# Output projection of a half chunk by seven block products, with shared row buffers and a new first chunk

## The chip, the cores and the metric

The kernel runs on one core of a Trainium2 chip, as one launch. The metric is device time in microseconds; three runs of the kernel before took 1395.66, 1396.66 and 1398.48 us, median 1396.66 us.

## The reference

The input x is 8 sequences of 1024 rows with 512 features, all float32. The reference does one attention sublayer and one feed-forward sublayer, each with a layer norm before and after and a residual:

```python
Q, K, V = heads(ln(x) @ Wq.T + bq), ...        # 16 heads of 32 columns
scores = Q @ K.T / sqrt(32) - (i - j)          # causal; the decay falls by 1 a row
out = softmax(scores) @ V @ Wo.T + bo          # <- the projection that is changed
x = x + ln(out)
xh = ln(x) @ H                                 # Hadamard, 512 x 512
xq = round(xh / s) * s                         # 4 bits, s from the row's maximum
x = x + ln(xq @ ternary(W).T)
```

The output projection is 8192 rows by 512 by 512, plain float32.

## The kernel before

Because the decay falls by 1 per row, only the own block of 128 keys and the block before it matter, and the fast path `band()` keeps only these (a general path stands behind a flag that the data decides). The work is cut into 16 chunks of 512 rows; a chunk has four tiles of 128 rows and two halves of 256 rows. Three kinds of work run side by side:

- **Attention units.** A chunk has eight, one per half and group of four heads. A unit is `scores` (TensorE into the four PSUM banks of `s`, L571, and four exponentials on ScalarE, L585), `mask` and `add_keys` (GpSimd, L596 and L610), `values` (TensorE into the single bank `av`, L626 and L637) and `divide` (VectorE, L655 to L660), which writes four heads of `oT`, the transposed attention output of the half.
- **Q, K and V of the next chunk.** Class `Projections`. Each of the three is already done as a two-by-two block product with seven instead of eight block multiplications (the Strassen-Winograd scheme): `Weight.combine` and `replace` make the weight combinations once, `Projections.combine` makes four combinations `T` of the input on GpSimd per chunk, `product` does one of the seven (L417, four matmuls of 128x256), `drain` adds it to what it belongs to (mostly VectorE, L447 to L470).
- **The rest of a tile.** Generator `rest`, 64 times: the output projection (`project`, L153, four matmuls of 128x512 into `o_ps`), the addition of the bias on VectorE (`y`, L187), its statistics, `x1` (L194), the Hadamard transform (`u` and `w` on VectorE, L198 to L203, four transposes `wT` on TensorE, L210, then `h_ps`, L218), the quantisation (`sc`, `isc`, `qf`, `qi`, L238 to L248), transposes `qiT` (L255), the ternary matmul `f_ps` (L153), statistics and the second residual on GpSimd (L285). `norm_in` is the same kind of generator for the first layer norm of chunks to come (`xc`, `xn`, `xnT`, L133 to L146).

The order is written out by hand. One turn of the loop over `u` handles two units, five or six of the 21 products, one tile's norm and the first and second part of one rest each (`rest_a`, `rest_b`). The engines take their instructions in this order. Three PSUM banks (`held`, `one`, `two`, chosen by `bank`) serve products, projections and transposes; the same bank is used again only after its content was read. A row buffer with `bufs=1` is likewise written only after its last reader.

A float32 matmul appears in the profile as two matmul records, called passes below. Before the loop, the first chunk's V, K and Q are computed by plain products of 128x512 (`project_v`, `project_qk`), while VectorE and GpSimd prepare the weights (`prepare`, `Weight.combine`).

Of the kernel before, what the change touches and what calls it, by code (L numbers as in the profile page):

```python
# [40 lines left out]
def sandwich_kernel(  # L41
# [88 lines left out]
    def norm_in(pools, row0, xnT, t, name):  # L130
# [6 lines left out]
        xn = pools.row.tile([P, D], F32, tag="xn", name=f"xn_{name}", bufs=1)  # L137
# [29 lines left out]
    def rest(pools, n, row0, oT, warm=(0, 0, 0), last=False):  # L167
# [13 lines left out]
        xr = row.tile([P, D], F32, tag="xr", name=f"xr_{n}", bufs=2)  # L181
        nc.sync.dma_start(xr, xf[row0, :])
        yield
        ps = project(pools, f"o_{n}", oT, lambda k: wo_sb[:, k, :])
        yield
        y = row.tile([P, D], F32, tag="y", name=f"y_{n}", bufs=1)
        nc.vector.tensor_tensor(y, ps, bo2, ALU.add)  # L187
# [9 lines left out]
        u = row.tile([P, D], F32, tag="u", name=f"u_{n}", bufs=1)  # L197
# [13 lines left out]
        wT = row.tile([P, KD, P], F32, tag="wT", name=f"wT_{n}", bufs=1)  # L211
# [33 lines left out]
        qf = row.tile([P, D], F32, tag="qf", name=f"qf_{n}", bufs=1)  # L245
        nc.scalar.activation(qf, xh, AF.Identity, bias=round_col, scale=isc)
        qi = row.tile([P, D], BF16, tag="qi", name=f"qi_{n}", bufs=1)
# [8 lines left out]
        qiT = row.tile([P, KD, P], BF16, tag="qiT", name=f"qiT_{n}", bufs=1)  # L256
# [47 lines left out]
    def band():  # L304
# [11 lines left out]
        class Chunk:  # L316
            def __init__(self, at):
                self.at = at
                self.b, self.c = divmod(at, NCHUNK)
                self.n = f"{self.b}_{self.c}"  # L320
                self.rests = []
# [54 lines left out]
        class Projections:  # L376


            ORDER = (1, 2, 6, 7, 5, 4, 3)

            def __init__(self, ch, before):
                self.ch, self.before, self.done, self.undrained = ch, before, 0, []
                ch.qT = big.tile([P, KD, CT], F32, tag="qT", name=f"qT_{ch.n}")
                ch.kT = big.tile([P, KD, CT], F32, tag="kT", name=f"kT_{ch.n}")
                ch.v = big.tile([P, TPC, D], F32, tag="v", name=f"v_{ch.n}")

            def combine(self, which, engine=nc.gpsimd):
# [4 lines left out]
                if which == 0:  # L392
# [4 lines left out]
                    self.parts = {1: b11, 2: b21, 3: b22, 5: t[:, 0], 6: t[:, 1]}  # L397
                elif which == 1:
                    nc.gpsimd.tensor_tensor(self.t[:, 2], b22, b12, ALU.subtract)
                    self.parts[7] = self.t[:, 2]  # L400
                else:
                    nc.gpsimd.tensor_tensor(self.t[:, 3], self.t[:, 1], b21, ALU.subtract)
                    self.parts[4] = self.t[:, 3]
# [18 lines left out]
            def drain(self):  # L422
# [11 lines left out]
                if which == 1:  # L434
                    self.u = row.tile([P, HB, HW], F32, tag="u2", name=f"u2_{name}", bufs=2)
# [69 lines left out]
            def shift(self):  # L505
# [5 lines left out]
                nc.gpsimd.tensor_scalar(shift, shift, -SLACK, -0.5, ALU.mult, ALU.add)  # L511
                nc.gpsimd.tensor_scalar(shift, shift, ROUND, None, ALU.add)
                nc.gpsimd.tensor_scalar(shift, shift, ROUND, None, ALU.subtract)
                ch.bias = small.tile([P, 2, 2], F32, tag="bias", name=f"bias_{ch.n}")
                nc.gpsimd.tensor_scalar(ch.bias, decay_cols, shift, None, ALU.add)
# [14 lines left out]
        class Unit:  # L530
# [118 lines left out]
            def divide(self):  # L649
# [8 lines left out]
                rn = row.tile([P, nblk, HD], F32, tag="rn", name=f"rn_{self.n}", bufs=1)  # L658
# [15 lines left out]

        def start_rest(ch, t):
# [10 lines left out]
                left == 1,  # L686
            )

# [8 lines left out]
        weights = [Weight(w, n) for w, n in ((wq_sb, "wq"), (wk_sb, "wk"), (wv_sb, "wv"))]  # L697

# [7 lines left out]
        ch.kT = big.tile([P, KD, CT], F32, tag="kT", name=f"kT_{ch.n}")  # L706
        ch.qT = big.tile([P, KD, CT], F32, tag="qT", name=f"qT_{ch.n}")
        ch.v = big.tile([P, TPC, D], F32, tag="v", name=f"v_{ch.n}")
# [19 lines left out]
        def squares_of_q(o0, o1):  # L728
            nc.scalar.activation(sqq[:, o0:o1, :], ch.qT[:, o0:o1, :], AF.Square)
# [9 lines left out]
        first = Projections(ch, None)  # L739
        prep = prepare(pools, wf_sb)  # L740
        ahead_steps = {0: "01", 1: "02", 2: "0", 3: "132", 4: "1", 5: "23", 6: "2", 7: "3", 8: "3"}
        for i in range(3 * KD):
            if i % 2 or not i:
                for t in ahead_steps.get(i, ""):
                    next(ahead_norms[int(t)])
            which, o = divmod(i, KD)
            if which == 0:
                project_v(pools, wv_sb, ch.v, ch.xnT, o, ch.n)
            elif which == 1:
                project_qk(pools, "k", wk_sb, bk_sb, ch.kT, ch.xnT, o, ch.n)  # L750
            else:
                project_qk(pools, "q", wq_sb, bq_sb, ch.qT, ch.xnT, o, ch.n)
            if i == 0:
# [3 lines left out]
            elif i == 1:  # L757
                transposed(3)
            elif i == KD - 1:
                prepare_q(wq_sb)  # L760
                nc.gpsimd.tensor_tensor(bqk_step[:, 0], bq_sb[:, HB:], bq_sb[:, :HB], ALU.subtract)
                nc.gpsimd.tensor_tensor(bqk_step[:, 1], bk_sb[:, HB:], bk_sb[:, :HB], ALU.subtract)
                weights[2].combine()
                weights[2].replace()
                weights[1].combine()
            elif i == 2 * KD - 1:
                weights[0].combine()
                weights[1].replace()
                sqk = squares(ch, "k", ch.kT)
                sqq = row.tile([P, KD, CT], BF16, tag="sq", name=f"sqq_{ch.n}", bufs=1)  # L770
            elif i == 2 * KD:
                ch.mk = largest_of(ch, "k", norms_of(ch, "k", sqk))
            elif i == 2 * KD + 2:
                squares_of_q(0, HB)
            if i and i % 2 == 0:
                for t in ahead_steps.get(i, ""):
                    next(ahead_norms[int(t)])
            if i in (KD, 6, 2 * KD):
                next(prep)
        squares_of_q(HB, KD)  # L780
        next(prep)
        next(prep)
        ch.mq = largest_of(ch, "q", norms_of(ch, "q", [sqq[:, o, :] for o in range(KD)]))
        first.multiply()
        next(prep)
        first.shift()
        next(prep)
        weights[0].replace(nc.vector)
# [22 lines left out]
        def bank(at):  # L811
            pools.ps_m.named = at

# [5 lines left out]
        for at, ch in enumerate(chunks[:-1]):  # L819
# [7 lines left out]
            for u in range(0, 2 * NG, 2):  # L827

                new = Unit(ch, before, u)
                new.scores()  # L830
                if u == 0:
                    proj.combine(0, nc.gpsimd if at else nc.vector)
                if unit:
                    unit.values()
                    unit.divide()
                unit = new
                steps(rest_a, 1)
                if u >= 4:
                    proj.square()
# [5 lines left out]
                norm = next(norms_due)  # L845
                steps(norm, 1)
# [7 lines left out]
                if u == 0:  # L854
                    proj.combine(1)
                rest_a = next(rests_due) if at or u >= 4 else None
                bank(one)
                steps(rest_a, 1)
                bank(two)
                steps(rest_b, 1)  # L860
                steps(rest_a, 1)
# [4 lines left out]
                new = Unit(ch, before, u + 1)  # L866
                new.scores()
                unit.values()
# [4 lines left out]
                steps(rest_b, 1)  # L873
# [3 lines left out]
                if u == 0:  # L877
                    proj.combine(2)
                steps(rest_a, 1)
                proj.drain()  # L880
                steps(rest_b, 1)
                new.add_keys()
                if u < 6:
                    unit.divide()
                bank(one)
                steps(norm, 1)
                bank(two)
                proj.product()
                proj.drain()
# [3 lines left out]
                if u == 6:  # L893
# [11 lines left out]
                    held, two = two, held  # L905
                else:
# [9 lines left out]
                steps(rest_a, 2)  # L916

# [252 lines left out]
    def prepare(pools, wf_sb):  # L1170
# [4 lines left out]
        nc.vector.tensor_reduce(ws, w, AX.X, ALU.add, apply_absolute_value=True)  # L1175
# [5 lines left out]
        diag = row.tile([P, KD, P], F32, tag="u", name="wdiag", bufs=1)  # L1181

        def ternary(k):
            below = row.tile([P, D], F32, tag="y", name=f"below_{k}", bufs=1)
            nc.vector.tensor_scalar(below, w[:, k, :], lo[:, k : k + 1], None, ALU.is_lt)
            tern = row.tile([P, D], BF16, tag=("qi", "qiT")[k % 2], name=f"tern_{k}", bufs=1)
            nc.vector.scalar_tensor_tensor(
                tern, w[:, k, :], hi[:, k : k + 1], below, ALU.is_gt, ALU.subtract
# [4 lines left out]
            return tern  # L1193

        def transposed(k, tern):
            pt = pools.ps_m.tile([P, KD, P], BF16, tag="pm", name=f"ternT_ps_{k}")
            for i in range(KD):
                nc.tensor.transpose(pt[:, i, :], tern[:, i * P : (i + 1) * P], ident_bf)
            nc.vector.tensor_copy(ternT[:, :, k * P : (k + 1) * P], pt)

        terns = [ternary(k) for k in range(2)]
        yield
        for k in range(2):
            transposed(k, terns[k])
        terns += [ternary(k) for k in range(2, KD)]
        yield
        nc.vector.tensor_copy(had0_sb, had_sb)
        nc.vector.memset(had0_sb[:, 0:1], 0.0)
        bvw = row.tile([P, KD, P], F32, tag="wT", name="bvw", bufs=1)
        nc.vector.tensor_copy(bvw, bvT_sb.unsqueeze(2).to_broadcast([P, KD, P]))  # L1210
# [4 lines left out]
        yield  # L1215
        for k in range(2, KD):
            transposed(k, terns[k])
        yield
        ps = pools.ps_m.tile([P, D], F32, tag="pm", name="bo2_ps")
# [59 lines left out]
```

## Time and profile before

| | us |
|---|---|
| median of three runs | 1396.66 |
| the profiled execution's own time | 1396.07 |
| its span, first to last instruction | 1394.3 |
| first `s` of the loop / last turn of the loop ends | 61.94 / about 1296 |

| engine | busy us | share |
|---|---|---|
| PE | 1363.4 | 98% |
| DVE | 1015.7 | 73% |
| POOL | 892.0 | 64% |
| ACT | 681.2 | 49% |

PE is TensorE, DVE is VectorE, ACT is ScalarE and POOL is GpSimd. Busy time of PE counts a matmul from its start to its modelled end, and consecutive matmuls overlap, so the distance from one start to the next tells more than the mean duration. The mean granted TensorE clock is 0.995.

### The profile page before, as it was taken

Reading aid. Unit: us, or ns where it says so; the run is one execution under the profiler, and the core shown is the slowest. Engines: PE = TensorE matmul, PEld = TensorE weight load, DVE = VectorE, ACT = ScalarE, POOL = GpSimd, SP = SyncE. Lnnn points to the kernel's source line nnn. Section 1 sums busy time; section 2 is a strip of 40 time slices with the busy share of each in tenths; the row PEclk is TensorE's granted clock in tenths of the full one; section 3 lists DMA queues with packets and bytes.
Section 4 is the critical chain, followed back from the end, with each engine's and each line's share of the span. In section 5 each row is a group of like instructions: output and inputs, shape, how many; then the busy total and the mean of one; then the engine's idle time right before and its main releaser. Section 6 shows DMA issues by size and latency. Waiting matters only on the chain.

```text
span 1394.3 us, 35003 instructions
## 1 busy us (share of the span) xinstructions
PE 1363.4 (98%) x14504; PEld 967.5 (69%) x14504; DVE 1015.7 (73%) x2167; ACT 681.2 (49%) x1176; POOL 892.0 (64%) x1280
## 2 busy tenths in 40 slices
PE   9999999999999999999999999999999999999895
PEld 5577777777767777767776777777776777766553
DVE  5467777777777776777777777877777777777675
ACT  3345454545445455554545545445544545535442
POOL 4565758576576767658676676757757666665434
PEclk9999999999999999999999999999999999999998
DMA  6010011011011011011011011011101101000010
GB/s 228 8 47 24 24 47 46 24 47 47 24 47 47 24 47 47 32 39 47 30 41 46 25 47 47 28 43 47 40 31 47 47 24 47 25 23 32 32 39 33
DMA packets 31750, 58.23 MB, mean 42 GB/s; under 512 B 4064, under 2 KB 4448, under 8 KB 31584
## 3 DMA queue, kind: packets, MB, share of 16 engines
q1 hardware_dynamic: 30720, 54.87, 11.4%
q8 instruction: 116, 1.90, 0.5%
q10 hardware_dynamic: 864, 1.05, 0.2%
q14 instruction: 50, 0.41, 0.1%
HBM read 39.13 MB, written 16.78 MB: 40 GB/s over the span
## 4 chain that ended last, share of the span: by engine, by line


## 5 line engine op out<-in xcount | busy, mean ns | idle before, releaser
L585 ACT ACTIVATE pr<-s,bias 128x512 f32<-128x512 f32 (+1 forms) x512 | 295.3, 660 | 138.5 <-PE s L571 138.5
L610 POOL TENSOR_TENSOR both<-pr 128x1024 f32<-128x1024 f32 (+1 forms) x120 | 250.5, 2088 | 5.2
L153 PE MATMUL o_ps<-wo_sb,oT 128*128 128x512 f32 x512 | 236.1, 604 | 0.6
L596 POOL TENSOR_SCALAR_AFFINE_SELECT pr<-pr 128x1024 f32<-128x1024 f32 x128 | 150.0, 1172 | 108.2 <-ACT pr L585 103.8
L153 PEld LDWEIGHTS o_ps<-wo_sb,oT 128*128 128x128 f32 x512 | 93.2, 192 | 95.2 <-issue 92.5
L187 DVE TENSOR_TENSOR y<-o_ps,bo 128x512 f32<-128x512 f32 x64 | 44.2, 691 | 150.5 <-PE o_ps L153 150.5
L626 PE MATMUL av<-pr,v 128*32 128x128 f32 (+1 forms) x2816 | 130.7, 316 | 1.8 <-DVE oT L660 1.8
L571 PE MATMUL s<-qT,kT 32*64 32x192 f32 (+2 forms) x5632 | 119.9, 285 | 1.5 <-ACT pr L585 1.5
L571 PEld LDWEIGHTS s<-qT,kT 32*64 32x64 f32 x5632 | 99.8, 131 | 31.0 <-issue 21.6
L141 ACT ACTIVATE xn<-xc,nmr,rstd_n 128x512 f32<-128x512 f32 x60 | 48.8, 814 | 140.0 <-POOL nmr L139 140.0
L119 POOL TENSOR_SCALAR rstd_a<-mv_a 128x1 f32<-128x1 f32 x64 | 13.9, 217 | 142.7 <-DVE mv_a L127 141.5
L226 ACT ACTIVATE wT<-h_ps 128x512 f32<-128x512 f32 x64 | 38.2, 597 | 133.8 <-PE h_ps L218 133.8
L626 PEld LDWEIGHTS av<-pr,v 128*32 128x32 f32 x2816 | 74.9, 110 | 35.4 <-issue 1.8
L212 ACT COPY wT<-wT_ps 128x512 f32<-128x512 f32 x64 | 37.5, 585 | 123.4 <-PE wT_ps L210 123.4
L238 DVE TENSOR_REDUCE sc<-h_ps 128x1 f32<-128x512 f32 x64 | 44.1, 689 | 63.8 <-ACT wT L226 63.8
L119 POOL TENSOR_SCALAR rstd_c<-mv_c 128x1 f32<-128x1 f32 x64 | 14.7, 229 | 116.1 <-DVE mv_c L127 116.0
L285 POOL TENSOR_TENSOR y<-y,x 128x512 f32<-128x512 f32 x63 | 80.6, 1279 | 1.3 <-ACT y L284 1.3
L637 PE MATMUL av<-both,ones 128*32 128x256 f32 x960 | 74.2, 381 | 0.5 <-POOL both L614 0.5
L218 PEld LDWEIGHTS h_ps<-had_sb,wT 128*128 128x128 f32 x512 | 66.8, 192 | 6.2 <-ACT wT L212 3.3
L218 PE MATMUL h_ps<-had_sb,wT 128*128 128x128 f32 x512 | 68.1, 276 | 2.1 <-ACT wT L212 2.1
L153 PE MATMUL f_ps<-ternT,qiT 128*128 128x512 bf16 x256 | 66.2, 382 | 2.4 <-ACT qiT L257 2.4
L146 ACT COPY xnT<-xnT_ps 128x512 f32<-128x512 f32 x60 | 35.2, 586 | 56.8 <-PE xnT_ps L145 56.8
(213 smaller groups left out, 3100.7 us busy)
## 6 DMA issues: line engine op xcount, KB each, us to landing
xr<-in_x SPq DMA_DIRECT2D x64, 256.0 KB, 2.9
out<-y SPq DMA_DIRECT2D x63, 256.0 KB, 2.0
xc<-in_x SPq DMA_DIRECT2D x60, 256.0 KB, 2.7
wv_sb<-in_wvT ACTq DMA_DIRECT2D x4, 256.0 KB, 5.1
x<-in_x SPq DMA_DIRECT2D x4, 256.0 KB, 4.9
wk_sb<-in_wkT SPq DMA_DIRECT2D x1, 1024.0 KB, 6.7
wq_sb<-in_wqT SPq DMA_DIRECT2D x1, 1024.0 KB, 9.0
wf_sb<-in_wf SPq DMA_DIRECT2D x1, 1024.0 KB, 10.7
```

The lines of the kernel that those rows point to most:

```text
L141: nc.scalar.activation(xn, xc, AF.Identity, bias=nmr, scale=r)
L153: nc.tensor.matmul(ps, lhs(k), rhs(k), start=(k == 0), stop=(k == KD - 1))
L187: nc.vector.tensor_tensor(y, ps, bo2, ALU.add)
L218: nc.tensor.matmul(xh[:, k * P : (k + 1) * P], wT[:, k, :], had_sb if k else had0_sb, start=True, stop=True,)
L238: nc.vector.tensor_reduce(sc, xh, AX.X, ALU.max, apply_absolute_value=True)
L285: nc.gpsimd.tensor_tensor(y2, y2, x1, ALU.add)
L571: nc.tensor.matmul(s[half * hp : (half + 1) * hp, hh, column[which] + c0 : column[which] + c1], kc.kT[hsl, g, k0 : k0 + hp], ch.qT[hsl, g, ...
L585: nc.scalar.activation(pr[:, :, r0:, own, cols], s5[:, :, r0:, own, cols], AF.Exp, bias=ch.bias[:, own, h : h + 1],)
L596: nc.gpsimd.affine_select(out=own, in_=own, compare_op=ALU.is_ge, fill=0.0, base=0, pattern=[[0, HPG], [0, 2], [1, P]], channel_multiplier=-1,
L610: engine.tensor_tensor(self.both[:, :, r0:], pr[:, :, r0:, 0, :], pr[:, :, r0:, 1, :], ALU.add)
L626: nc.tensor.matmul(av[hh * HD : (hh + 1) * HD, 0, qc : qc + w], kc.v[:, at, h * HD : (h + 1) * HD], pr[:, hh, sc : sc + w], start=(at_part ...
L637: nc.tensor.matmul(av[hh * HD : (hh + 1) * HD, 1, :], ones[:, :HD], self.both[:, hh].rearrange("p r c -> p (r c)") if own is None else sel ...
```

## The change

Both tiles of a half are now projected together. The half's `oT` is 512 by 256, so as blocks it is two by two (two halves of the features, two tiles), and `wo` is two by two as well. A class `Output` makes four combinations of `oT`: `t0`, `t1` and one in place of a block on GpSimd, one in place on VectorE. It does seven products of two matmuls of 128x256, and puts them in pairs into one PSUM bank: 1 and 2, 6 and 7, 4 and 5, then 3 alone. Nine additions of 128x256 on VectorE per half lay them into `y` of the two tiles. All seven products stand in the first half of every second turn (`pair`), where the old order had one tile's projection; one of the Q, K and V products goes from each `pair` turn to the turn after it. 29 of the 32 halves are done like this; the last six tiles keep the plain projection, for which `wo` is loaded a second time.

```diff
+            def combine(self, which):
+                if which == 0:
+                    self.t0 = row.tile([P, HB, P], F32, tag="t0", ...)
+                    nc.gpsimd.tensor_tensor(self.t0, self.b12, self.b11, ALU.subtract)
+                elif which == 1:
+                    self.t1 = row.tile([P, HB, P], F32, tag="t1", ...)
+                    nc.gpsimd.tensor_tensor(self.t1, self.b22, self.t0, ALU.subtract)
+                    nc.gpsimd.tensor_tensor(self.b12, self.b22, self.b12, ALU.subtract)
...
+                else:
+                    nc.vector.tensor_tensor(self.b21, self.t1, self.b21, ALU.subtract)
...
+            def drain(self, which):
...
+                if which == 1:
+                    add(self.u, ps, bo2[:, left], ALU.add)
+                elif which == 2:
+                    add(self.y[0][:, left], ps, self.u, ALU.add)
+                elif which == 6:
+                    add(self.u, ps, self.u, ALU.add)
+                    add(self.u3, self.u, bo2[:, right], ALU.add)
+                elif which == 7:
+                    add(self.u3, ps, self.u3, ALU.add)
+                elif which == 4:
+                    add(self.y[0][:, right], ps, self.u3, ALU.add)
+                elif which == 5:
+                    add(self.y[1][:, right], ps, self.u3, ALU.add)
+                    add(self.u, ps, self.u, ALU.add)
+                else:
+                    add(self.y[1][:, left], ps, self.u, ALU.add)
```

`rest` takes the finished `y` instead of projecting. Rows with a short life share buffers: `u`, `wT` and `qf` one, `qi` and `qiT` one, `xn` and `w` one, `sumT` and `rn` one; `xr`, `u2` have one buffer instead of two, and the load of `xr` is issued one step later.

```diff
-        xn = pools.row.tile([P, D], F32, tag="xn", name=f"xn_{name}", bufs=1)
+        xn = pools.row.tile([P, D], F32, tag="w", name=f"xn_{name}", bufs=1)
...
-        xr = row.tile([P, D], F32, tag="xr", name=f"xr_{n}", bufs=2)
+        yield
+        xr = row.tile([P, D], F32, tag="u3" if last else "xr", name=f"xr_{n}", bufs=1)
         nc.sync.dma_start(xr, xf[row0, :])
-        yield
-        ps = project(pools, f"o_{n}", oT, lambda k: wo_sb[:, k, :])
-        yield
-        y = row.tile([P, D], F32, tag="y", name=f"y_{n}", bufs=1)
-        nc.vector.tensor_tensor(y, ps, bo2, ALU.add)
+        if not made:
+            ps = project(pools, f"o_{n}", oT, lambda k: wo_sb[:, k, :])
+        yield
+        if made:
+            y = made()
+        else:
...
```

The loop over `u`, in its first half:

```diff
                 if unit:
                     unit.values()
                     unit.divide()
+                if out:
+                    out.combine(1)
...
                 bank(one)
-                steps(rest_a, 1)
-                bank(two)
-                steps(rest_b, 1)
-                steps(rest_a, 1)
+                if out:
+                    out.products(1, 2)
+                    steps(rest_a, 1)
+                    out.drain(1)
+                    out.drain(2)
+                    bank(held)
+                    steps(rest_b, 1)
+                    out.combine(2)
+                    steps(rest_b, 1)
+                    bank(two)
+                    out.products(6, 7)
+                    out.drain(6)
+                    out.drain(7)
+                    bank(one)
+                    out.products(4, 5)
+                    out.drain(4)
+                    steps(rest_a, 1)
+                    out.drain(5)
+                    bank(held)
+                    steps(norm, 1)
+                    bank(two)
+                    out.products(3)
+                    out.drain(3)
+                else:
+                    if not pair:
+                        proj.product()
+                        proj.drain()
...
```

In the second half of a turn `new.add_keys()` (GpSimd) goes ahead of a step of `rest_b`, and in a `pair` turn the transposes `xnT` are no longer there and one product is left out. The products of Q, K and V come in the order 1, 2, 6, 7, 5, 3, 4. `Projections.combine(0)` on GpSimd moves behind the first unit's `add_keys`. `wo.combine` and `wo.replace` (GpSimd) come in the first chunk, between turns.

Ahead of the loop, K and Q of the first chunk are done by seven products each, with the input combinations on VectorE; the absolute sums of the ternary weights go from one VectorE reduction to four ScalarE instructions; the bias row `bvw` is summed over the four blocks of features on GpSimd (seven instructions of 128x512), so that one matmul in place of four is left; and the ternary preparation is spread between the products, one or two VectorE instructions at a time:

```diff
+        for i in range(kinds):
+            first.product()
+            first.drain()
...
+            next(prep)
+        sqk = squares(ch, "k", ch.kT)
...
```

## The prediction

> **What bounds the kernel now.** I read first the page (busy times), then the groups of instructions with shapes kept apart, then who waited for whom on PE and DVE, and last the timeline of one turn in the steady part.
>
> ```profile
> PE 1363.4 (98%) x14504; PEld 967.5 (69%) x14504; DVE 1015.7 (73%) x2167; ACT 681.2 (49%) x1176; POOL 892.0 (64%) x1280
> ...
> L153 PE MATMUL o_ps<-wo_sb,oT 128*128 128x512 f32 x512 | 236.1, 604 | 0.6
> L417 PE MATMUL q_ps<-xnT,wq_s 128*128 128x256 f32 x120 | 28.4, 379 | 0.0
> ```
>
> TensorE is busy 98% of the span and the output projection is its largest group. So TensorE's work is the bound, if it really works in that time. The waits say that it does:
>
> ```profile
> PE qiT_ps L255 <- DVE qi L248: 4.4, 6, 1.1
> PE f_ps L153 <- ACT qiT L257: 2.4, 3, 1.0
> ...
> DVE y L187 <- PE o_ps L153: 150.5, 60, 5.7
> ```
>
> The longest entry of PE is 4.4 us in all, while VectorE waits 150.5 us for the output projection. Off TensorE there is slack; its largest piece lies just where the change puts new VectorE work.
>
> ```profile
> 591.91 1.89 PE L417 MATMUL k_ps<-T,wk_s 128*128 128x256 f32 x8
> 593.64 0.39 PE L255 MATMUL qiT_ps<-ident_bf,qi 128*128 128x128 bf16 x4
> ...
> 574.43 3.65 PE L153 MATMUL o_ps<-wo_sb,oT 128*128 128x512 f32 x8
> 577.91 1.03 PE L153 MATMUL f_ps<-ternT,qiT 128*128 128x512 bf16 x4
> ```
>
> From start to next start, a product of 8 passes of 256 columns takes 1.73 us (216 ns a pass), a tile's projection of 8 passes of 512 columns 3.48 us (435 ns a pass). Half the columns cost half the time.
>
> **The change, part by part.**
>
> *Output projection.* Per half before: 2 x 3.48 = 6.96 us. After: seven products of 4 passes, 7 x 1.73/2 = 6.06 us. It saves 0.90 us a half, 29 halves: **-26.2 us**. Here a rule speaks against it. The Trainium skill ("TensorE: Matmul & The Clock Gate", Back-to-back issue gap, and LDWEIGHTS) says that in a stream of weight loads and matmuls the spacing is set by both, and that a load takes its columns / 1.2 GHz, about 107 ns for 128. There are 28 passes with a load each in place of 16. If the 12 additional loads lay open, that would be 12 x 0.107 = 1.28 us, more than the 0.90 saved, and the sum would be +11 us. The trace decides against it for this shape: PEld is busy 967.5 us beside PE, and the 256-column products, which reload for every pass too, keep 216 ns. I take the row.
>
> *New additions on VectorE.* Per half, two `y` of 128x512 (691 ns) go, nine additions of 128x256 and one combination come. Near rows: `oT`, 128x256 with one PSUM input, 424 ns; `u`, two SBUF inputs, 452. Ten x 0.43 - 1.38 = +2.9 us a half, +85 us in all: DVE goes from 1016 to about 1100 of 1372 us, 80%. On GpSimd three combinations of 128x256, half of `T`'s 1281 ns: +1.9 us a half, +56 us, so POOL comes to about 69%. Neither becomes the bound by its sum. They cost something only where a chain gets longer than TensorE's work beside it, so I lay out a `pair` turn from the durations above (s 0.92, av 1.44, products 1.83 then 1.73, transposes 0.44, bf16 transposes 0.22, f 0.96, h 0.98), zero at the end of its first `s`:
>
> av to 1.44, two Q/K/V products to 5.00, qiT to 5.22, products 1 and 2 to 6.95, f to 7.91, 6 and 7 to 9.64, 4 and 5 to 11.37, xnT to 11.81, 3 to 12.68, s to 13.60, av to 15.04, product to 16.87, **wT at 16.87**, product to 19.04, h to 20.02, s to 20.94, and in the next turn av to 22.38, two products to 25.94, **qiT at 25.94**.
>
> *The chain to `wT`.* Before, it runs from the end of `o_ps`:
>
> ```profile
> 578.12 0.69 DVE L187 TENSOR_TENSOR y<-o_ps,bo 128x512 f32<-128x512 f32 x1 [2.52 <-PE o_ps L153]
> 578.84 0.69 DVE L126 BATCH_NORM_STATS2 st_a<-y 128x6 f32<-128x512 f32 x1
> ...
> 580.73 0.75 DVE L194 SCALAR_TENSOR_TENSOR x<-y,rstd_a,xr 128x512 f32<-128x512 f32 x1 [0.33 <-POOL rstd_a L120]
> 581.52 0.42 DVE L198 TENSOR_TENSOR u<-x 128x256 f32<-128x256 f32 x1
> ...
> 582.31 1.21 DVE L202 TENSOR_TENSOR w<-u 128x256 f32<-128x256 f32 x1
> 583.45 0.41 DVE L203 TENSOR_TENSOR w<-u 128x256 f32<-128x256 f32 x1
> ```
>
> It ended at 583.86, 0.93 us ahead of `wT` at 584.79. After, the drain of product 4 starts at 11.37 + 0.21 = 11.58; drain 0.46 and statistics 0.83 to 12.87; the three additions of products 5 and 3 to about 14.0, while POOL makes `rstd_a` (0.21 + 0.56 and two hand-overs, about 13.9); x1 0.79, u 0.79 to 15.6; w 0.35 and 0.41 to 16.4. Slack 0.5 us at u = 0; at u = 4 the norm matmuls (0.33) add to the cover. The 1.21 above is the thing to weigh: that `w` ran beside the mask (581.85, 1.40 us instead of 1.11). The skill ("SBUF — State Buffer", Who interferes with whom) says that a VectorE instruction with two SBUF inputs and a GpSimd instruction that reads SBUF exclude each other for the whole instruction. By the rule, `w`, `u`, the new `ou3` and the combination could each lose up to a whole `add_keys`, 2.38 us; by the group's mean (`w` 816 ns against 410 alone) it is 0.4 each. The mask of that time starts only when the four exponentials (2.41) are through, at about 16.15, when `w` is nearly done. The chain before had 0.93 us of slack here and in other turns still came late (626.00 where 625.70 was due, 648.36 where 648.10), so with half the slack I take 0.25 us late on average.
>
> *The chain to the next `qiT`.* TensorE's second half of a `pair` turn is short now: 7.3 us from s to s, 9.5 before. There POOL has mask 1.1, `add_keys` 2.4 (to 19.7), then the `rstd_c` chain, which the change puts behind `add_keys`, to about 21.2. ACT applies it (0.8) and does the exponentials only after that: 22.0 to 24.5, then `qf` 0.7, `qi` 0.5 to 0.8: 25.9 against `qiT` at 25.94. Before, the exponentials began 0.54 after `s`, here 1.1. I take 0.25 us late.
>
> *The turn after it* waits little: its first half is 8.8 us instead of 10.5, but VectorE's chain to the second `wT` has `y` ready from before. `w` shares `xn`'s buffer, so it cannot start before `xnT` is transposed (33.5 on this clock) and ends at 34.3 to 35.1 against 35.21. I take 0.2. The other new sharings follow readers that are already done on the same queue; SP's later `xr` (2.9 us to land) is issued some 10 us ahead of `x1`.
>
> Sum of waits: (0.25 + 0.25 + 0.2) x 29 = 20 us. Against it stand the waits at the same two places before, which these replace: over the whole timeline, what follows `wT` and `qiT` starts later than by their medians by 7.8 and 5.3 us, 13 in all. Net **+7 us**, bounds -10 (all of them gone, few new) and +20.
>
> *Ahead of the loop.* K and Q: 8 x 3.45 = 27.6 us become 14 x 1.73 = 24.2; the bias row 2 x 1.82 becomes 0.9. That is -6 us of TensorE's work, but now VectorE sets the pace there: per K product a drain (0.7 to 1.4) and a ternary step (`below` 0.99, `tern` 0.97 + `wdiag` 0.62); K alone is 5.1 + 11.5 us of VectorE for 13 us of TensorE, and the first drain starts late, since ScalarE's four absolute sums (about 4 us from 25.1) stand ahead of product 1's bias. Followed product by product, K ends near 43.9 instead of 40.6, Q near 56.6, the first `s` at about 60.7 instead of 61.94, and the first exponentials, which wait for `bias`, at the same 63. In the first turn q7 waits for a `T` on POOL by about 1 us. I take **-1 us**, bounds -5 and +4.
>
> *The rest.* The last chunk's order is unchanged; `wo`'s second load has a whole chunk to land. `wo.combine` and `replace` (seven POOL instructions near 1.3 us) stand in two turns: 0 to +2, counted in the bounds.
>
> Sum on the profiled execution: 1396.07 - 26.2 + 7 - 1 = 1375.9. That execution stands 0.6 below the median of the runs shown; so 1376.5, say **1376**.
>
> **The rivals.**
>
> *The chains eat most of it.* For: three places have a slack under 0.5 us by my clock, and VectorE goes to 80%. Against: before, a chunk (578.87 to 662.75, 83.9 us) lost 1.4 us to late starts, a third of a microsecond a tile. If every half loses 0.2 to 0.6 us more than I took, the time is 1376 + 29 x 0.2 to 0.6: 1382 to 1393.
>
> *Slower: VectorE is blocked by GpSimd in the `pair` turn.* One mechanism: in the stretch from product 4 to `wT` one of `u` and `w` (two SBUF inputs) meets the start of `add_keys` and waits out its 2.38 us, in every half. Its price is 2.38 less 0.5 slack, 1.9 us a half, 29 x (1.9 - 0.90) = +29, so 1425. It decides from 1.0 us a half on (0.90 plus the 2.8 us that make 0.2%). For it: 1.21 instead of 0.41 above. Against: `add_keys` starts at about 17.3, a microsecond after `w`; VectorE would have to be 1 us late already.
>
> *No change.* If the 256-column products took more than half, as in the loads' rule by two thirds, the time would stay at 1393 to 1399. The Q, K and V rows speak against it. That the change does not do what it says is excluded by its instructions: 232 matmuls of 128x512 fewer, 406 of 128x256 more.
>
> *More than I say.* If the net of the waits is zero and the start gives 3 to 5 us: 1366 to 1368.
>
> **How the numbers follow.** My forecast (1366 to 1382, with the case of more than I say) 0.63; chains eat most (1382 to 1393) 0.19; no change 0.05; slower 0.13. A difference of 0.2% (2.8 us) is about what a measurement of this kernel can tell from none. Faster 0.82, same 0.05, slower 0.13. The range that leaves out no more than 2 in 10 reaches from 1366 to 1395.
>
> **What would show it.** Right: `o_ps` falls from 236 to about 200 us busy with 24 plain matmuls left; PE stays at 97 to 98%; PE's waits for `wT`'s `w` and for `qi` rise, to some 20 us together. Wrong: PE's waits or late starts at `wT`, `qiT` or `xnT` over 40 us together, a `w` that averages over 1.2 us, a pass of the new products over 225 ns, or a first `s` after 66 us.

## The result, and the profile after

The changed kernel takes **1499.07 us** (median; 1498.31 to 1501.39) against 1396.87 for the kernel before on the same chip: ratio 1.0733, 95% interval 1.0719 to 1.0746. It is 102 us slower, where I had forecast 20 faster. Its profiled execution has a span of 1496.9 us.

The busy times of the page, engine by engine with share of the span and number of instructions:

```profile
PE 1360.3 (91%) x14831; PEld 1055.2 (70%) x14894; DVE 1192.8 (80%) x2419; ACT 680.1 (45%) x1181; POOL 983.8 (66%) x1379
```

TensorE is busy no longer than before (1363.4 us), but that is 91% of the span in place of 98%. It waits. The waits of PE for `wT` in the kernel before, and the longest four now (who waited for whom; us in total, times, longest):

```profile
PE wT_ps L210 <- DVE w L203: 1.1, 1, 1.1
PE wT_ps L210 <- DVE u_v L453: 1.0, 3, 0.6
```

```profile
PE wT_ps L215 <- DVE w L208: 47.6, 36, 2.2
PE wT_ps L215 <- DVE u_v L460: 32.4, 15, 2.7
PE wT_ps L215 <- DVE w L207: 19.6, 30, 1.0
PE qiT_ps L260 <- DVE qi L253: 4.4, 6, 1.0
```

Three entries of `wT`, 99.6 us, stand where the kernel before had 2.3 (the two shown and one of 0.2); `qiT` is as it was. The groups with shapes kept apart (busy us, mean ns of one | idle before it), the additions `w` of the kernel before first:

```profile
L202 DVE TENSOR_TENSOR w<-u 128x256 f32<-128x256 f32 x64 | 52.2, 816 | 2.3
L203 DVE TENSOR_TENSOR w<-u 128x256 f32<-128x256 f32 x64 | 47.8, 747 | 0.0
```

```profile
L557 PE MATMUL o_ps<-wo_sb,oT 128*128 128x256 f32 x464 | 112.0, 384 | 0.2 <-DVE u_k L463 0.2
L557 PE MATMUL o_ps<-wo_s,t 128*128 128x256 f32 x232 | 59.5, 379 | 0.0
L557 PE MATMUL o_ps<-wo_s,oT 128*128 128x256 f32 x116 | 30.7, 387 | 0.3 <-DVE ou L585 0.2
...
L207 DVE TENSOR_TENSOR w<-u 128x256 f32<-128x256 f32 x64 | 81.0, 1265 | 23.4 <-PE xnT_ps L145 18.0 <-ACT pr L662 0.5
L208 DVE TENSOR_TENSOR w<-u 128x256 f32<-128x256 f32 x64 | 77.3, 1208 | 0.0
```

The seven products cost nearly what I said. The three groups are busy for 202.2 us, but busy times of consecutive matmuls overlap; from start to next start, a pass takes 216 ns (median) and 224 ns (mean, some short waits included), 181.7 us in all. But the same additions that make `w` average 1265 and 1208 ns; they were 816 and 747 before, and take 0.41 to 0.42 us at their shortest. Why, the timeline of one `pair` turn (u = 4) shows (start, us, engine, line, operation, out<-in; in brackets the engine's idle time before it, and what ended that):

```profile
1004.78 1.11 POOL L673 TENSOR_SCALAR_AFFINE_SELECT pr<-pr 128x1024 f32<-128x1024 f32 x1 [2.03 <-ACT pr L662]
1004.87 1.30 DVE L207 TENSOR_TENSOR w<-u 128x256 f32<-128x256 f32 x1
1005.97 2.39 POOL L687 TENSOR_TENSOR both<-pr 128x1024 f32<-128x1024 f32 x1
1006.08 2.56 DVE L208 TENSOR_TENSOR w<-u 128x256 f32<-128x256 f32 x1
1006.31 0.30 PE L215 MATMUL wT_ps<-ident,w 128*128 128x128 f32 x1 [0.52 <-DVE w L207]
...
1008.70 0.90 PE L215 MATMUL wT_ps<-ident,w 128*128 128x128 f32 x3 [2.09 <-DVE w L208]
...
1009.40 3.12 PE L424 MATMUL k_ps<-T,wk_sb 128*128 128x256 f32 x8
```

The mask holds up the first `w` (1.30 us). This `w` gets its turn between the two GpSimd instructions, and `add_keys` (the `both` row) holds up the second for its whole length: 2.56.

Additions of the same size that read one input from PSUM, the memory that TensorE writes its results to, are not held up. In the first half of the same turn:

```profile
994.59 2.36 POOL L687 TENSOR_TENSOR both<-pr 128x1024 f32<-128x1024 f32 x1
996.19 0.42 DVE L579 TENSOR_TENSOR y<-o_ps,ou 128x256 f32<-128x256 f32 x1
```

All 29 of these `y` take 424 to 426 ns, and 22 of them start inside an `add_keys`. So most of the new additions were not caught; what was caught are mainly `u` and `w`, with both inputs in SBUF, and these stood in the kernel before as well.

In a turn without output products (u = 6) it is `u` that is caught, one `u` behind the mask and the next behind `add_keys`:

```profile
1025.75 1.20 POOL L673 TENSOR_SCALAR_AFFINE_SELECT pr<-pr 128x1024 f32<-128x1024 f32 x1 [1.45 <-ACT pr L662]
1026.02 1.21 DVE L203 TENSOR_TENSOR u<-x 128x256 f32<-128x256 f32 x1
...
1027.03 2.40 POOL L687 TENSOR_TENSOR both<-pr 128x1024 f32<-128x1024 f32 x1
1027.15 2.57 DVE L204 TENSOR_TENSOR u<-x 128x256 f32<-128x256 f32 x1
...
1031.36 0.63 PE L215 MATMUL wT_ps<-ident,w 128*128 128x128 f32 x4 [2.44 <-DVE u_v L460]
```

Here the wait bears the name of `u_v`. That drain is short; it frees the bank that `wT` goes into, and it stands behind `u` and `w` in VectorE's queue. In the kernel before, GpSimd's queue at the same place was:

```profile
581.85 1.40 POOL L596 TENSOR_SCALAR_AFFINE_SELECT pr<-pr 128x1024 f32<-128x1024 f32 x1 [0.23 <-ACT pr L585]
584.77 0.23 POOL L119 TENSOR_SCALAR rstd_c<-mv_c 128x1 f32<-128x1 f32 x1 [1.52 <-DVE mv_c L127]
...
586.24 1.26 POOL L610 TENSOR_TENSOR both<-pr 128x512 f32<-128x512 f32 x1
```

`rstd_c` waits for statistics that VectorE makes *after* `w`. Standing between the mask and `add_keys`, it kept `add_keys` away from `u` and `w` in all turns of the two chunks compared below, without saying so. The diff exchanges two lines, `steps(rest_b, 1)` and `new.add_keys()`, and that guard is gone.

How long each stretch of a chunk is tells where the 102 us lie. From the start of one unit's `s` to the next on PE's timeline, mean of two chunks in the steady part, in us (the last two columns are experiments below):

| stretch | before | after | e1_keys_back | e9_gate |
|---|---|---|---|---|
| u = 0, first half (output products) | 10.48 | 13.62 | 13.78 | 13.80 |
| u = 0, second half | 9.98 | 8.64 | 8.16 | 7.35 |
| u = 2, first half | 10.45 | 9.18 | 9.69 | 9.58 |
| u = 2, second half | 9.29 | 10.33 | 9.29 | 9.29 |
| u = 4, first half (output products) | 10.99 | 13.60 | 13.60 | 13.60 |
| u = 4, second half | 9.50 | 11.32 | 8.41 | 7.54 |
| u = 6, first half | 10.92 | 8.88 | 9.34 | 9.23 |
| u = 6, second half | 11.63 | 14.80 | 11.92 | 11.92 |
| a chunk | 83.2 | 90.4 | 84.2 | 82.3 |

Over all 15 chunks the loop takes 109 us more than before; the first `s` starts at 58.07 instead of 61.94, 4 us earlier, and what follows the loop is 2 us shorter. 109 - 4 - 2 = 103, the difference of the two spans. The change moves work from second halves of `pair` turns to first halves, so the loss is seen best against e9_gate, which has the same work on TensorE: its first halves are not shorter (46.2 us a chunk against 45.3), its second halves take 36.1 us in place of 45.1. All of the loss is in second halves, the ones with `wT`.

Part of it is TensorE's clock. In the timeline above, the product behind `wT` takes 2.95 us to the next start, not 1.73. The windows view shows the granted clock (the number before DMA's share) and, first, how long TensorE was busy. Two stretches of 3.41 us here, and two at the same place one chunk earlier, where the waits are as long and the product takes 1.73:

```profile
1005.04:1008.45 3.41, 1.05 (x5) 0.46 (x3) 3.41 (x2) 0.00 (x0) 3.24 (x2) 1.00 0.00 0
1008.45:1011.86 3.41, 3.16 (x9) 2.71 (x10) 2.98 (x8) 0.58 (x1) 1.25 (x4) 0.50 0.02 5
...
916.29:919.70 3.41, 1.99 (x9) 1.28 (x7) 3.31 (x4) 0.61 (x2) 2.64 (x2) 1.00 0.00 0
919.70:923.11 3.41, 2.21 (x12) 2.01 (x13) 3.31 (x7) 0.59 (x1) 1.54 (x3) 1.00 0.00 0
```

Between the first and the last `s`, the stretches at half clock all last 3.41 us, and within a trace they begin whole multiples of 3.41 us from one another. Laid on this grid, the ten traces of this case give: of the stretches with TensorE busy for under 1.5 us, all 27 are followed by one at half clock; of those with 1.5 to 1.75 us, 6 of 21; of the some 3800 with more, none. So it is not the length of a wait alone that counts, but how much of it falls between two lines of the grid: at 1005 us most of it, one chunk earlier about half on either side.

The changed kernel has 15 of these stretches at half clock, the kernel before 1. Each costs at most half of 3.41 us, so the clock is at most 14 x 1.71 = 24 us of the 102.

### The profile page after: what moved, and what is told of

It is laid out like the page before. It is cut to its first block, busy times and chain, and to the rows that moved or that the text cites. A ratio compares the mean times of both kernels' runs of the same rounds, so it can differ in the third digit from the quotient of the medians.

```text
span 1496.9 us, 36476 instructions
## 1 busy us (share of the span) xinstructions
PE 1360.3 (91%) x14831; PEld 1055.2 (70%) x14894; DVE 1192.8 (80%) x2419; ACT 680.1 (45%) x1181; POOL 983.8 (66%) x1379
## 4 chain that ended last, share of the span: by engine, by line
## 5 line engine op out<-in xcount | busy, mean ns | idle before, releaser
L215 PE MATMUL wT_ps<-ident,w 128*128 128x128 f32 x256 | 51.8, 299 | 99.6 <-DVE w L208 47.6
L215 PEld LDWEIGHTS wT_ps<-ident,w 128*128 128x128 f32 x256 | 29.3, 144 | 129.5 <-DVE w L208 56.6
L557 PE MATMUL o_ps<-wo_sb,oT 128*128 128x256 f32 x464 | 112.0, 384 | 0.2 <-DVE u_k L463 0.2
L207 DVE TENSOR_TENSOR w<-u 128x256 f32<-128x256 f32 x64 | 81.0, 1265 | 23.4 <-PE xnT_ps L145 18.0
L557 PEld LDWEIGHTS o_ps<-wo_sb,oT 128*128 128x128 f32 x464 | 85.8, 190 | 11.8 <-DVE oT L548 0.4
L208 DVE TENSOR_TENSOR w<-u 128x256 f32<-128x256 f32 x64 | 77.3, 1208 | 0.0
L235 POOL TENSOR_SCALAR rstd_b<-var 128x1 f32<-128x1 f32 x64 | 12.3, 192 | 98.6 <-ACT wT L231 98.5
```

The source lines that it names most:

```text
L207: nc.vector.tensor_tensor(w[:, :, 0, :], u4[:, :, 0, :], u4[:, :, 1, :], ALU.add)
L208: nc.vector.tensor_tensor(w[:, :, 1, :], u4[:, :, 0, :], u4[:, :, 1, :], ALU.subtract)
L215: nc.tensor.transpose(pt[:, k, :], w[:, k // 2, k % 2, :], ident)
L557: nc.tensor.matmul(ps[:, at, :], self.parts[i][:, k, :], wo.parts[i][:, k, :], start=(k == 0), stop=(k == HB - 1),)
```

## The experiments

The theories at the start: the *lock* (`add_keys`, moved ahead, meets `u` and `w`); *VectorE's load* (nine more additions a half make it late whatever GpSimd does); the *shared buffer* (`w` waits for `xnT`); and the *clock*, as an amplifier.

### GpSimd's order put back

```diff
                 proj.drain()
-                new.add_keys()
                 steps(rest_b, 1)
+                new.add_keys()
```

> The changed kernel with one line moved: in the second half of a turn of the loop, new.add_keys() stands behind steps(rest_b, 1) again, as it did before, so that on GpSimd the rstd_c chain (which waits for statistics queued on VectorE behind w) stands between the mask and add_keys. Lock theory (VectorE's u and w, two SBUF inputs, are shut out by add_keys when it follows the mask directly): both lines of w fall from 1265 and 1208 ns to under 850, PE's waits and late starts at wT from about 116 us to under 25, the time to 1372 to 1395 us, so nearly all of the loss of 102 us goes. VectorE-load theory (the nine additions a half make VectorE late whatever GpSimd does, 80% busy): the order on GpSimd does not matter, wT stays late by over 80 us, the time stays over 1470. Shared-buffer theory (w cannot start before xnT has been transposed out of the same buffer): also no change, over 1470.

Measured: 1406.68 us against 1396.34 before, ratio 1.0074 (1.0057 to 1.0091). 92 of the 102 us go with one line. `w` falls to 733 and 535 ns. That is the lock theory's side, though the time came out 12 us above its range. PE's waits:

```profile
PE wT_ps L215 <- DVE w L207: 13.4, 23, 0.7
PE wT_ps L215 <- DVE w L208: 6.3, 7, 2.1
...
PE av L714 <- POOL both L687: 5.3, 21, 0.3
```

Two things are left: `wT` still waits, now mostly for the `w` that the mask holds up, and `av`'s product with ones waits for the later `add_keys`.

### The order alone, in the kernel before

```diff
                 proj.drain()
-                steps(rest_b, 1)
                 new.add_keys()
+                steps(rest_b, 1)
```

> The kernel before with only new.add_keys() moved ahead of steps(rest_b, 1) in the second half of a turn; nothing of the output projection is changed. Lock theory: u and w meet add_keys here too, w goes from 816 and 747 ns to over 1100, wT starts late by some 60 to 110 us in all, the time is 1450 to 1500 us. It comes out below that if the chain to wT, which without the additions is shorter by about 1 us, is through before add_keys starts. VectorE-load theory and shared-buffer theory: no change, 1392 to 1402.

Measured: 1433.25 us, ratio 1.0261 (1.0244 to 1.0278). The order alone costs 37 us, and the load and the shared-buffer theories, which allow none, fall as the whole cause. My 60 to 110 was too much. At u = 4 the shorter chain is through before `add_keys`; at u = 2 a `w` is caught in every other chunk, but TensorE does not wait for it. Most of the loss is at u = 6, whose second half grows by some 1.9 us, and a little at u = 0. At u = 6:

```profile
984.55 2.40 POOL L610 TENSOR_TENSOR both<-pr 128x1024 f32<-128x1024 f32 x1
984.78 2.45 DVE L202 TENSOR_TENSOR w<-u 128x256 f32<-128x256 f32 x1
...
988.22 0.66 PE L210 MATMUL wT_ps<-ident,w 128*128 128x128 f32 x4 [2.17 <-DVE u_v L453]
```

With the run before, this makes a table of four: neither 0, the rest of the change with the old order +10, the order alone +37, both +102. The two multiply each other, for in the changed kernel VectorE's chain comes later and TensorE's second half is shorter, so that in the two chunks looked at `add_keys` catches a `u` or `w` in seven of eight turns, and TensorE waits in all of them.

### GpSimd busy, but reading nothing

The edit, shortened:

```diff
-                engine.tensor_tensor(self.both[:, :, r0:], pr..., pr..., ALU.add)
+                for _ in range(2):
+                    nc.gpsimd.memset(self.both, 1.0)      # second half of a turn only
```

> The changed kernel, its order kept, but the add_keys of the second half of a turn is two memsets of its result: GpSimd works for about as long in the same place and writes SBUF, but reads nothing (the sums of the softmax's rows are left out for those units). Lock theory, in the form that it is GpSimd's reading that shuts VectorE out: w falls to under 850 ns beside a busy GpSimd, and the time to 1375 to 1410. Rival: what costs is that GpSimd is occupied there, and that rstd_c and what follows on its queue come later. Then the time stays over 1470.

Measured: 1387.54 us, ratio 0.9938 (0.9921 to 0.9954), with the change's own order. In the u = 4 turn:

```profile
850.68 1.11 POOL L673 TENSOR_SCALAR_AFFINE_SELECT pr<-pr 128x1024 f32<-128x1024 f32 x1 [2.03 <-ACT pr L662]
850.77 1.30 DVE L207 TENSOR_TENSOR w<-u 128x256 f32<-128x256 f32 x1
851.73 1.96 POOL L689 MEMSET both<- 128x1024 f32 x2
851.99 0.41 DVE L208 TENSOR_TENSOR w<-u 128x256 f32<-128x256 f32 x1
```

The mask, which reads SBUF, still holds up the first `w`. Beside the memsets, GpSimd as occupied as it was, the second takes 0.41 us. So it is the reading, not the occupation and not the order of GpSimd's results. The means of `w` fall to 734 and 501 ns, near those of e1_keys_back.

### The idle stretch filled

```diff
-                WARM.get(left, (0, 0, 0)),
+                WARM.get(left, (16, 0, 0) if t < 2 else (0, 0, 0)),
```

> The changed kernel with 16 dummy transposes (about 1.8 us) ahead of the wT transposes of the first two tiles of a chunk, those whose wT comes 2.0 to 3.3 us late in the turns u = 4 and u = 6. If part of the loss is that TensorE runs at half clock after an idle stretch (the product behind wT takes 2.9 us to the next start instead of 1.73), the idle stretch is now filled, the product takes 1.73 to 1.9, and the kernel is 15 to 30 us faster than the changed one: 1469 to 1484. If the slow product has another cause (its own operands, or the bank), the dummy work only lies in the wait or adds to it: 1495 to 1530.

Measured: 1519.24 us (1513.69 to 1526.48), 20 above the changed kernel. The remedy fails, for a reason that the waits name: at u = 6 the dummies themselves stand and wait for the bank, and only then add their time.

```profile
PE wT_ps L213 <- DVE u_v L460: 32.4, 15, 2.7
```

At u = 4 they do lie in the wait, and the second half there takes 10.57 us in both chunks in place of 10.55 and 12.09. But the low clock then turns up at u = 0 of every other chunk, behind two waits of 0.61 and 1.08 us that fall into one stretch of the grid (1.73 us busy):

```profile
978.08:981.49 3.41, 1.73 (x9) 1.10 (x8) 3.41 (x4) 0.40 (x1) 2.71 (x3) 1.00 0.00 0
981.49:984.90 3.41, 3.41 (x12) 2.95 (x11) 2.59 (x8) 0.19 (x1) 1.25 (x4) 0.50 0.00 0
```

What decides among the stretches between 1.5 and 1.75 us stays open. Where the waits at `wT` are short (e1, e3, and e6 to e9) the mean granted clock is 0.996 to 0.998, so the low clock goes with the waits; it is not a cause of its own.

### What is left: later mq, sooner keys

Built on e1_keys_back. The order in the second half is now (shortened; the lines at the old places are left out):

```diff
                 steps(rest_a, 1)        # x1, u, w
+                if u < 6: steps(rest_b, 1)      # statistics of y2, rstd_c
                 proj.drain()
+                if u == 4: proj.largest()       # mq, was ahead of the mask
+                if u == 6: steps(rest_b, 1)
                 new.add_keys()
```

> The kernel of e1_keys_back with two more moves in the second half of a turn: the statistics of y2 (and so rstd_c on GpSimd) come ahead of the drain of the product except at u = 6, so that add_keys starts about 0.7 us sooner; and at u = 4 the reduction for mq stands behind w instead of ahead of x1. In e1_keys_back TensorE waits 5.3 us for add_keys (both), and the first halves of turns are 0.3 to 0.7 us longer than in e3_no_read, 2.3 us in two chunks; and wT comes 0.87 us late at u = 4. If the late add_keys and the reduction are these causes: waits for both under 1 us, u = 4 late by under 0.4, 1380 to 1392 us, ahead of the kernel before. If add_keys, now sooner again, meets u or w, or if GpSimd's later rstd_b is the cause: 1400 to 1415.

Measured: 1400.67 us, ratio 1.0042 (1.0028 to 1.0057): by the ratios some 4 to 5 us faster than e1_keys_back, not the 15 to 25 that I expected. `av`'s wait for `both` falls off the list, as expected. But the mq move was a mistake:

```profile
PE wT_ps L215 <- DVE mq L345: 22.2, 15, 1.6
```

The norms lie in the bank that `wT` needs next; read later, they hold it up 15 times. What left ahead of `x1` came back as a wait for the bank. The time lies at the lower end of the second range of the expectation, 1400 to 1415, but for this reason and not for one of the two named there.

### The mask behind w, by way of rstd_c

On top of e6_reorder, shortened:

```diff
+                if not pair: new.mask()
                 steps(rest_a, 1)
                 if u < 6: steps(rest_b, 1)
+                if pair: new.mask()
```

> e6_reorder, and in the pair turns the mask also stands behind the rstd_c chain on GpSimd, which waits for statistics that VectorE makes after w. So neither the mask nor add_keys can meet u and w in those turns. If the mask locks w out as add_keys does (w 1.14 and 1.30 beside it, 0.41 alone), w L207 falls from 733 ns to about 550, wT in the pair turns is late by under 0.3 instead of 0.9, and the time falls by another 10 to 20 us against e6_reorder: 1365 to 1380. Rival: add_keys ends 0.8 us later, and av's product with ones waits for it: the gain goes, 1385 to 1400.

Measured: 1406.14 us, ratio 1.0083 (1.0067 to 1.0100), with the mq mistake still in it. That is 5 us slower than e6_reorder and above both ranges of the expectation. `w` is free of the lock (438 ns), and the second half at u = 0 falls from 8.26 to 7.34 us in the chunk compared. But the rival's wait is there:

```profile
PE av L714 <- POOL both L687: 5.8, 7, 0.8
PE av L714 <- POOL both L691: 5.7, 8, 0.7
```

The first half of u = 2 grows from 9.37 to 10.53. GpSimd's chain of `rstd_c`, mask, `add_keys` is too long if it all starts only after the statistics.

### Three additions fewer

```diff
-                    out.drain(5)
+                    out.y[1] = out.y[0]
...
-                    out.drain(3)
```

> The kernel of e1_keys_back without the drains of products 5 and 3 (three additions of 128x256 a half fewer; the second tile of a half takes the first one's y, so half of the output's rows are computed from the wrong rows). VectorE-load theory for what is left of the loss in e1_keys_back (10 us over the kernel before, wT 0.9 us late in the pair turns): without some 1.3 us of VectorE's work a half, u and w come earlier, wT is late by under 0.3 in the pair turns, and the time falls by 15 to 30 us: 1377 to 1392. If x1 waits for something else there (rstd_a, the exponentials, the mask beside w): late by 0.7 to 0.9 as in e1_keys_back, 1400 to 1408.

Measured: 1407.10 us, ratio 1.0082: e1's time, though some 1.3 us of VectorE's work in every half is gone. The u = 0 turn tells why:

```profile
1240.29 0.75 DVE L199 SCALAR_TENSOR_TENSOR x<-y,rstd_a,xr 128x512 f32<-128x512 f32 x1 [0.99 <-POOL rstd_a L120]
...
1242.21 1.33 DVE L208 TENSOR_TENSOR w<-u 128x256 f32<-128x256 f32 x1
```

`x1` then waits 0.99 us for `rstd_a`, so VectorE gets ahead by little, and the mask (at 1241.91) catches the second `w`, where in the same turn of e1 it catches the first. In the two chunks of the steady part the mask catches the same `w` as in e1, for 1.33 and 1.11 us. VectorE's load is not what is left in e1; the mask is.

### The gate

From e6, with mq back where the change had it. In a `pair` turn GpSimd copies one column of `w` before the mask (shortened):

```diff
         nc.vector.tensor_tensor(w[:, :, 1, :], ..., ALU.subtract)
+        if gate:      # tiles whose w lies in a pair turn
+            nc.gpsimd.tensor_copy(after_w, w[:, 1, 1, P - 1 :])
...
                 if u >= 4: proj.largest()
+                if not out: new.mask()
                 steps(rest_a, 1)
+                if out: new.mask()
+                if u < 6: steps(rest_b, 1)
                 proj.drain()
+                if u == 6: steps(rest_b, 1)
                 new.add_keys()
```

> The changed kernel with the order of e6_reorder (add_keys behind rstd_c, the statistics of y2 ahead of the drain for u below 6), the mq reduction where the change had it, and in the pair turns the mask behind w: GpSimd first copies one column of w (a gate of some 0.2 us that waits for VectorE), then masks, then makes rstd_c, then adds the keys. So no GpSimd instruction that reads SBUF at length can stand beside u or w there, and add_keys ends some 0.5 us sooner than in e7_mask_behind_w. Lock theory with both GpSimd instructions in it: the second halves of the pair turns, from s to s, fall from 8.25 and 8.40 us (e1_keys_back) to about 7.4 and 7.6, the first halves after them stay at 9.4 and 8.9, two chunks take about 163 us against 166.5 before, and the time is 1360 to 1375: the forecast of the change comes true with GpSimd's order repaired. Rival: the later mask or rstd_c delays the product of av with ones, or the exponentials behind them, by as much, as in e7_mask_behind_w: 1385 to 1405.

Measured: **1377.16 us** against 1396.01 before, ratio 0.9863 (0.9846 to 0.9879). It beats both kernels, the changed one by 122 us, but lies 2 us above the range of the expectation. The busy times, the group of `w`, and the u = 4 turn:

```profile
PE 1329.7 (97%) x14831; PEld 1036.7 (75%) x14894; DVE 1066.6 (78%) x2419; ACT 682.6 (50%) x1181; POOL 978.1 (71%) x1408
```

```profile
L207 DVE TENSOR_TENSOR w<-u 128x256 f32<-128x256 f32 x64 | 28.0, 438 | 23.4 <-PE xnT_ps L145 18.0 <-ACT pr L665 0.5
```

```profile
844.35 0.42 DVE L207 TENSOR_TENSOR w<-u 128x256 f32<-128x256 f32 x1
844.69 0.42 DVE L208 TENSOR_TENSOR w<-u 128x256 f32<-128x256 f32 x1
...
845.11 0.60 PE L218 MATMUL wT_ps<-ident,w 128*128 128x128 f32 x4
845.18 0.18 POOL L211 COPY gate<-w 128x1 f32<-128x1 f32 x1 [2.94 <-DVE w L208]
845.31 1.11 POOL L676 TENSOR_SCALAR_AFFINE_SELECT pr<-pr 128x1024 f32<-128x1024 f32 x1
```

`wT` follows its product at once; the second halves of the `pair` turns take 7.35 and 7.54 us. VectorE's instructions are the changed kernel's own, 2419 of them, but its busy time is 1066.6 us, not 1192.8: of the 126 us between them, 121 are in `u` and `w`, so that much of the "work" in the changed kernel was standing at the lock. And `w` still waits 18.0 us for `xnT`, as in the changed kernel, so the shared buffer is not the cause either. (Giving `xn` a buffer of its own wasn't tried. What the gate and the earlier statistics each bring was not taken apart.)

## Why the prediction was wrong, point by point

*The output projection, -26.2 us: right, a little too high.* From start to next start, the output projection takes 205.7 us with the 24 plain matmuls, where the kernel before took 228.6: 22.9 us less. The passes keep 216 ns, and the case against it (loads lying open) did not come. That case was sized with 107 ns a load, although the trace before shows 190 to 192 ns for such a load; they stay covered all the same. The sign that I named, `o_ps` at about 200 us busy, did not come, since it mixed spacing with busy time: 202.2 + 21.9 = 224.1 us busy.

*The start, -1 us: right in sign, small.* First `s` at 58.07 where I had 60.7; the trace gives 4 us.

*The chain to `wT`, 0.25 us late in the `pair` turn: the step that failed.* I wrote that the mask starts "when `w` is nearly done" and `add_keys` "at about 17.3", a microsecond behind it. What the runs show in place of 0.25 us is 2.61 at u = 4 (0.52 and 2.09 in the timeline above) and 1.31 on average at u = 0, and with GpSimd's old order the 99.6 us of waits at `wT` fall to 22.2. Two of the signs of being wrong that I had named came with it: over 40 us of waits, and a `w` above 1.2 us. Three things were wrong in my step. At u = 4 the reduction for mq (0.69 us) stands on VectorE ahead of `x1`; I had counted the norms as cover on TensorE and not as work on VectorE. A `w` caught by the mask ends just where `add_keys` begins, so a delay of half a microsecond does not cost half a microsecond, it costs the next lock as well: 1.30, then 2.56. And I sized the lock by the group's mean, 0.4 us, although those means were made under an order in which `add_keys` did not occur beside `w` in the steady part. The rule of the Trainium skill ("SBUF — State Buffer", Who interferes with whom) had the size right, a whole instruction, and also that only a reading GpSimd does it; the trace agrees with 2.56 us beside `add_keys` and 0.41 beside memsets. I had both sizes in front of me and took the smaller.

*"The turn after it waits little", 0.2 us: also wrong, by the same omission.* The exchange of `add_keys` and the `rstd_c` step is in every turn, and I followed it only in the `pair` turn, and there only for what it does to `qiT`. At u = 2 and u = 6 the second half grew by 1.04 and 3.17 us.

*The chain to the next `qiT`, 0.25 us: did not occur.* Its wait is 4.4 us in all, as before, and 4.5 in e9_gate, where no late `wT` gives it time; the first halves of u = 2 and u = 6, which hold that `qiT`, are the shortest of the four kernels in the table (9.18, 8.88).

*The rival on the slower side* had the mechanism and the place: one of `u` and `w` waits out `add_keys`. Its price, 1.9 us for a `pair` turn, was somewhat low (3.8 us at u = 4 between changed kernel and e9_gate, 1.3 at u = 0, on average 2.5). That it would hit the other two turns as well, with 4 us more a chunk, and bring the clock down, was missing: 1499 instead of 1425. The argument I held against it, that VectorE would have to be 1 us late already, was true; at u = 4, mq and the mask made it so.

*The sum itself* was that of another order. With GpSimd's instructions where hardly any can meet `u` or `w`, the same output products give 1377.2 us. That this is so near to 1376 is in part luck: in the loop e9_gate gains 12.8 us where I had 19 (26.2 less 7), and the start and what follows the loop, 3.5 and 1.9 us, make up for it.

What e9_gate leaves: three of its first halves are 0.2 to 0.4 us longer than the changed kernel's. `add_keys` ends later there than in the changed kernel, but whether that is the cause was not followed further.

## What to carry to other kernels

When a diff moves an instruction on GpSimd, ask what VectorE does at its new time with two inputs from SBUF, in every turn that has the line, not only in the turn that the change is about. A wait in another engine's queue may be the only thing that keeps two instructions apart, so look at what stood between them before it is moved; if they must not meet, make that explicit with an instruction that waits, even a copy of one column. And when a mean is lower than a lock's whole length, find out first whether the two met at all in that trace.

## What the runs showed of the hardware that I had not expected

Between two GpSimd instructions that read SBUF back to back, VectorE got just the one addition through that was waiting, and the next was held again: 1.30 then 2.56 us at u = 4, 1.21 then 2.57 at u = 6. An addition of the same size with one input in PSUM was never held: 424 to 426 ns, 22 times beside `add_keys`. A busy share rises with it (80% against 78%, and 1192.8 us against 1066.6 for the same instructions), so a VectorE that looks loaded may be one that is held. And a TensorE wait of 2 to 3 us can cost half the clock for the product that follows (2.95 us for 1.73). Whether it did was told, in these traces, by a fixed grid of 3.41 us: under 1.5 us of TensorE's work in one stretch, and the next one ran at half clock, 27 times of 27.
